# A recurrent mixer with a gated feed-forward branch: another order of transpositions, exponentials and output sums in the mixer's loop

## The chip, the cores and the metric

The kernel runs on one core of one Trainium2 chip, in float32. The metric is the device time of one launch in microseconds. Three runs of the kernel before took 1824.26, 1824.22 and 1823.35 us, so the median is 1824.22 us.

The engines are called as in the profile: PE is the matrix engine (PEld its weight loads), DVE the VectorE, ACT the ScalarE, POOL the GpSimd engine, and SP the engine that issues most DMAs. Each engine works through its own instructions in order; they wait for each other through semaphores.

## The reference

The input x has 4 batches of 256 tokens with 512 columns (1024 tokens). Cut to what matters:

```python
xn = layernorm(x)
# mixer: 128 heads of 64, 8 groups, state 128
zxbcdt = xn @ in_proj_w.T                  # gate | x,B,C | dt
gate, xBC, dt = split(zxbcdt)
xBC = silu(causal_conv(xBC, conv_w, taps=4) + conv_b)
x_, B, C = split(xBC);  dt = softplus(dt + dt_bias);  A = -exp(A_log)
# per head: y[t] = sum_{s<=t} (C[t].B[s]) * exp(sum_{s<m<=t} A*dt[m]) * dt[s] * x_[s] + D * x_[t]
y = y * silu(gate)
y = y * rsqrt(mean(y*y over the group's 1024 columns) + 1e-5) * norm_w
s = y @ out_proj_w.T
# feed-forward on the same xn, ternary weights with a scale per row
f = (silu(xn @ gate_w.T) * (xn @ up_w.T)) @ down_w.T
return x + s * silu(f)
```

The reference computes the recurrence in chunks of 32 tokens; the kernel takes chunks of 128, two per batch.

## The kernel before

**Front.** The function `front` normalizes x, transposes it, computes the feed-forward branch in 28 iterations and stores it to DRAM. Between its products it feeds in "pieces", three per iteration: the dt rows, the scores C.B of all 8 groups (`bc_pieces`, stored to `scores`), and `early_pieces`. The latter loads the two projection weight tiles of one mixer tile, waits for four turns of the pieces, adds and subtracts their blocks on DVE (`combine_to`) and stores the sums to `early` in DRAM. It does so for EARLY = 7 tiles.

**Mixer.** The 8192 channels are 64 tiles of 128 channels (two heads each), eight tiles per group. The loop at L714 has 66 steps. Step i projects tile i, finishes the y of tile i-1, gates and squares tile i-2, and computes a part of the output projection of an older group. All instructions stand in an order written out by hand (`manual_schedule`), so that the order in the program is the order on each engine's queue.

The projection of a tile uses seven products of half size instead of eight (Strassen's scheme in Winograd's form). Its left factors are blocks of the two weight tiles and sums of them (s1, s2, s4, s3); its right factors are blocks of the normalized input and sums made once (`xc`). The results gather in three PSUM banks px, pq and pz (pool `ps_proj`, three buffers). The PE order in step i is a11 (px), s1 (pq), s2 (px), a12 (pz), s3 (px), then the first transposition group, a22 (px), s4 (pq), then the second transposition group. Between the px products ACT copies px away: to pz (L750), gT (L759), and the two halves of `xpad` (L771, L806). DVE adds pq to xpad (L795) and to gT (L808). The left sums of a tile come from `early` for the first seven tiles (L841) and from `combine_w` on DVE for later ones; both go into the one buffer of the pool `scp`.

For tile i-1, `decay_scan` (DVE, L560) and `decay_exp` (ACT, L563) make the decay matrices `m` of both heads from rows loaded with DMAs; `meet` (L566, L567) multiplies them with the scores. `values_0` transposes the first chunk of each batch into the PSUM tile `tp` and multiplies it twice on DVE (L580, first with dt, then with dt_tail); `values_1` does the same with the second chunk and one multiply (L589). Both take `tp` from pool `ps_t`, which has one buffer. `y_products` (L613) then forms y.

After the taps of the convolution (L181) comes its silu (L186). For tiles below LEAD = 6 it runs on ACT in the next step, after the copy on L750, followed by both exponentials; for later tiles it ends the step itself, with the first exponential after it. Exponential and silu need different tables on ACT, so each step loads a table twice.

**Output.** Four batches of a finished group are projected by seven products of quarter size each (`out_first`), four of them in an even step and three in the next odd one, from step 10 on. The left factors come from the stored tiles (`load_gated`, pool `yap`, two buffers), with four sums on DVE (`left_factors`, L649 to L652, one buffer `sy`). ACT scales each result into `sa` or `sb` (L724), and POOL adds them into `acc` in DRAM (L857 to L860). The right factors' sums (`right_factors`, `toms`) are spread over the steps with on = 7, 0 and 1. The last group is projected after the loop: DVE adds each product to the loaded sum (L890), `end` multiplies by the feed-forward branch, adds x and stores. The four left sums for the next batch follow the last `end` of a batch.

In steps 64 and 65 there is no projection any more; the gating, the output products and the y of tile 63 remain.

Of the kernel before, what the change touches and what calls it, by code (L numbers as in the profile page):

```python
# [50 lines left out]
P = 128  # L51
NB = 4
L = 256
NC = 2
# [20 lines left out]
LEAD = 6  # L75
EARLY = 7
# [5 lines left out]
def mixer_ffn(ctx: ExitStack, tc: tile.TileContext, x, in_w, conv_w, conv_b, dt_bias, a_log, d_col,  # L82
# [23 lines left out]
    scp = main.enter_context(tc.tile_pool(name="scp", bufs=1))  # L106
# [60 lines left out]
    def by_batch(v):  # L167
        return v.rearrange("p (b l) -> p b l", l=L)
# [20 lines left out]
    def front(pre, one_of, fp, f2, hp, wq):  # L189
# [251 lines left out]
        def early_pieces():  # L441
            for n in range(EARLY):
                w = wq.tile([P, 2, KT, P], F32, name="wq")
                for m, i in enumerate((n + 1, CT + n + 1)):
                    nc.sync.dma_start(w[:, m], in_w[i])
                for _ in range(4):
                    yield
                s = wq.tile([P, 4, KT // 2, P], F32, name="sq")
                yield from combine_to(s[:, 0], s[:, 1], s[:, 2], s[:, 3], w)
                nc.sync.dma_start(early[n], s)  # L450
                yield
# [84 lines left out]
    yap = main.enter_context(tc.tile_pool(name="yap", bufs=2, reuse_waits="tile"))  # L536
# [25 lines left out]
    def decay_exp(m):  # L562
        nc.scalar.activation(m, m, AF.Exp)  # L563
# [145 lines left out]
    with tc.manual_schedule():  # L709
# [3 lines left out]
        sqacc, rs, ya, outs = None, None, None, None  # L713
        for i in range(CT + 2):  # L714
# [4 lines left out]
            sums = []  # L719
# [5 lines left out]

            if i + 1 <= EARLY:
                w = wp.tile([P, 2, KT, P], F32, name="w")
                nc.sync.dma_start(w[:, 0], in_w[i + 1])
                nc.sync.dma_start(w[:, 1, 0:2], early[i, :, 3])
                nc.sync.dma_start(w[:, 1, 2:4], in_w[CT + i + 1, :, 2:4])  # L730
            elif i + 1 < CT:
                w = load_w(i + 1, CT + i + 1)
# [18 lines left out]
            if old and i - 1 < LEAD:  # L751
                conv_silu(i - 1, xTs[i - 1])
                decay_exp(ms[i - 1][0])
            if old:
                decay_exp(ms[i - 1][1])
            if here:
                product(pq, s1, t1, True)
                product(px, s2, t2, False)
                nc.scalar.copy(gT[:, HALF:], px)  # L759
                if i:  # L760
                    decay_scan(ms[i][0])
                product(pz, a12, x21, False)
# [23 lines left out]
            if og >= 0 and on % 2 == 0:  # L786
                ob, ya = on // 2, nxt
                left, sums = left_factors(ya)
                for make in sums:
                    make()  # L790
# [3 lines left out]
            if here:  # L794
                nc.vector.tensor_add(xpad_h[1], xpad_h[1], by_batch(pq))  # L795
            if old:
                vs = values_0(i - 1, xTs[i - 1])
            if og >= 0 and on == 0:
                rs = small.tile([P, NT], F32, name="rs2", bufs=2)
                nc.vector.reciprocal(rs, sd)  # L800
            for n, turn in ((wg, PER_G - 1), (og, 0), (og, 1)):
                if n >= 0 and on == turn:
                    toms[n].pop(0)()
            if here:
                product(px, a22, t4, False)
                nc.scalar.copy(xpad_h[0], by_batch(px))  # L806
                product(pq, s4, x22, False)
                nc.vector.tensor_add(gT[:, HALF:], gT[:, HALF:], pq)  # L808
            if old:
                vs.append(values_1(i - 1, xTs[i - 1]))  # L810
            if here:
                xTs[i] = xtp.tile([P, NB, L], F32, name="xT")
                last_tap(i, xTs[i], xpad)
            if here:
                nc.scalar.activation(gT[:, 0:HALF], pz, AF.Silu)
            if og >= 0:
                if on % 2 == 0:
                    sa = osp.tile([P, NC, HID], F32, name="sa")
                    sb = osp.tile([P, 3, HH], F32, name="sb")
                    outs = out_first(left, rights[og], leave)  # L820
                for n in range(4 - on % 2):
                    next(outs)
                    if here and n == 1:
                        nc.scalar.activation(gT[:, HALF:], gT[:, HALF:], AF.Silu)
            elif here:
                nc.scalar.activation(gT[:, HALF:], gT[:, HALF:], AF.Silu)
# [7 lines left out]
            if here:  # L834
# [12 lines left out]
                if i == 0:  # L847
                    decay_scan(ms[i][0])
                decay_scan(ms[i][1])
# [26 lines left out]
        yas = {0: nxt, 1: load_gated(G - 1, 1)}  # L876
# [8 lines left out]
        for b in range(NB):  # L885
# [14 lines left out]
            sums = []  # L900
            for n, _ in enumerate(out_first(left, rights[G - 1], leave_last)):
                if n == 4:
                    end(1, slice(HH, HID))
                if n == 5:
                    end(0, slice(0, HID))
            end(1, slice(0, HH))
            if b + 1 < NB:
                left, sums = left_factors(yas[b + 1])
                for make in sums:
                    make()  # L910
            if b + 2 < NB:
                yas[b + 2] = load_gated(G - 1, b + 2)
                whole[b + 2] = fetch(b + 2)
    main.close()
# [46 lines left out]
```

## Time and profile before

| what | value |
|---|---|
| median of three runs | 1824.22 us |
| the profiled execution's own time | 1825.28 us |
| its span, from first to last instruction | 1823.6 us |
| front | about 332 us |
| steps 2 to 5 of the mixer | 17.79 us each |
| steps 7 and 8 | 19.05 and 19.04 us |
| main steps, even and odd | 23.27 and 21.55 us |
| PE busy | 1744.5 us (96%) |
| DVE busy | 1451.8 us (80%) |
| ACT busy | 1072.9 us (59%) |
| mean granted PE clock | 0.99 |

Lines of the page's groups give the line of the program, the engine, the operation, output and inputs, and then busy time, mean duration and the idle time before it. A line of the timeline gives start, duration, engine, line and the number of merged instructions; the bracket at its end tells how long the engine stood idle before it, and what ended that. The step times are the distances between the starts of the copy on L750. Busy time of PE contains overlaps of one matmul with the next, so 96% busy doesn't mean that a matmul of 512 columns takes the 0.6 us of its row: four of them start every 1.72 us.

### The profile page before, as it was taken

What the parts mean: (1) busy time and instruction counts of PE and PEld (TensorE: products, weight loads), DVE (VectorE), ACT (ScalarE), POOL (GpSimd) and SP (SyncE); (2) the same over time, 40 slices, a digit from 0 to 9 for tenths busy, and PEclk for the clock granted to TensorE, in tenths of its full rate; (3) what the DMA queues carried; (4) which work ended last, traced back from release to release, by engine and by line L of the source; (5) the groups of instructions that cost most, each with busy time, mean ns of one, the idle gap of its engine ahead of it and who ended that gap; (6) DMA issues with size and microseconds to landing.
All of it is one profiled execution on the core that took longest, in us unless ns stands there. A gap on an engine that the chain in (4) does not pass through costs nothing.

```text
span 1823.6 us, 22452 instructions
## 1 busy us (share of the span) xinstructions
PE 1744.5 (96%) x8446; PEld 1113.5 (61%) x8446; DVE 1451.8 (80%) x1736; ACT 1072.9 (59%) x1419; POOL 198.8 (11%) x235
## 2 busy tenths in 40 slices
PE   6899899899899999999999999999999999999988
PEld 4566566545456666666666666666666666666676
DVE  5556657598898888888888888888888888888866
ACT  3543333477766666666666666666666666666630
POOL 2222112000000000111011101110111011101110
PEclk8999999999999999999999999999999999999989
DMA  6235443467646665766676667666767676767665
GB/s 202 66 131 173 145 145 132 151 218 207 211 150 213 199 199 181 211 200 197 183 213 199 193 186 210 196 188 197 204 197 200 183 205 196 202 182 202 176 181 169
DMA packets 161739, 337.05 MB, mean 185 GB/s; under 512 B 15072, under 2 KB 54752, under 8 KB 161632
## 3 DMA queue, kind: packets, MB, share of 16 engines
q1 hardware_dynamic: 139120, 283.19, 44.8%
q0 software_dynamic: 22512, 52.44, 16.5%
q8 instruction: 67, 1.10, 0.2%
q14 instruction: 40, 0.33, 0.1%
HBM read 232.55 MB, written 74.19 MB: 168 GB/s over the span
## 4 chain that ended last, share of the span: by engine, by line
PE 84%; DVE 8%; ACT 6%; issue 2%; DMA 1%; SPq 0%; DVEq 0%; ACTq 0%
PE px L173 27%; PE po L669 20%; PE pq L173 12%; PE py L613 9%; PE pz L173 6%; PE pp L279 4%; ACT xpad L771 2%; PE pf L287 2%; PE tp L572 1%; PE pg L432 1%; DVE cT L181 1%; ACT m L563 1%; PE pv L631 1%; DVE xT L181 1%; DVE m L560 0%
## 5 line engine op out<-in xcount | busy, mean ns | idle before, releaser
L173 PE MATMUL px<-xc,w 128*128 128x512 f32 x576 | 279.9, 608 | 23.5 <-ACT xpad L771 15.7
L560 DVE TENSOR_TENSOR_SCAN m<-m,after 128x1024 f32<-128x1024 f32 x128 | 291.9, 2282 | 0.0
L181 DVE SCALAR_TENSOR_TENSOR xT<-xpad,cw,xT 128x1024 f32<-128x1024 f32 x192 | 246.1, 1282 | 4.6
L173 PEld LDWEIGHTS px<-xc,w 128*128 128x128 f32 x576 | 103.4, 190 | 142.5 <-issue 97.2
L669 PE MATMUL po<-wo,ya 128*128 128x256 f32 x768 | 178.3, 382 | 0.0
L613 PE MATMUL py<-m,v 128*64 128x128 f32 x2048 | 160.6, 276 | 5.3 <-DVE v L589 5.3
L566 DVE TENSOR_TENSOR m<-m,gm 128x1024 f32<-128x1024 f32 x128 | 154.8, 1210 | 6.8 <-ACT m L563 6.8
L669 PEld LDWEIGHTS po<-wo,ya 128*128 128x128 f32 x768 | 142.5, 192 | 17.6 <-issue 0.4
L831 POOL DMA_DIRECT2D sqacc<-sq x55 | 48.3, 879 | 948.9 <-ACT sq L783 948.9
L173 PE MATMUL px<-xc,s 128*128 128x512 f32 x288 | 138.1, 602 | 13.4 <-ACT cpad L402 7.2
L173 PE MATMUL px<-xnT,w 128*128 128x512 f32 x288 | 141.8, 614 | 0.0
L173 PE MATMUL pq<-xc,s 128*128 128x512 f32 x288 | 135.4, 592 | 1.6 <-DVE xT L181 1.6
L173 PE MATMUL pq<-xnT,s 128*128 128x512 f32 x288 | 135.7, 593 | 0.5 <-DVE xpad L795 0.4
L563 ACT ACTIVATE m<-m 128x1024 f32<-128x1024 f32 x128 | 134.7, 1057 | 1.7 <-DVE m L560 0.9
L173 PE MATMUL pz<-xnT,w 128*128 128x512 f32 x288 | 135.3, 592 | 0.0
L613 PEld LDWEIGHTS py<-m,v 128*64 128x64 f32 x2048 | 116.9, 137 | 27.3 <-issue 19.7
L669 PE MATMUL po<-tw,sy 128*128 128x256 f32 x512 | 117.8, 382 | 2.8 <-DVE sy L649 1.4
L808 DVE TENSOR_TENSOR gT<-gT,pq 128x512 f32<-128x512 f32 x64 | 44.0, 688 | 83.4 <-PE pq L173 83.4
L795 DVE TENSOR_TENSOR xpad<-xpad,pq 128x512 f32<-128x512 f32 x64 | 43.8, 684 | 83.3 <-ACT xpad L771 83.1
L572 PEld LDWEIGHTS tp<-ident,xT 128*128 128x128 f32 x512 | 64.1, 141 | 75.0 <-issue 75.0
L669 PEld LDWEIGHTS po<-tw,sy 128*128 128x128 f32 x512 | 97.5, 191 | 18.6 <-DVE m L890 2.8
L620 DVE TENSOR_TENSOR yg<-py,gT 128x512 f32<-128x512 f32 x128 | 83.9, 678 | 28.6 <-PE py L613 28.6
(165 smaller groups left out, 3077.5 us busy)
## 6 DMA issues: line engine op xcount, KB each, us to landing
m<-rows SPq DMA_DIRECT2D x128, 512.0 KB, 6.3
w<-in_in_w SPq DMA_DIRECT2D x137, 256.0 KB, 6.7
mo<-rows SPq DMA_DIRECT2D x128, 256.0 KB, 7.0
gated<-yg SPq DMA_DIRECT2D x64, 512.0 KB, 8.2
ya<-gated SPq DMA_DIRECT2D x31, 1024.0 KB, 7.0
sqacc<-sq POOLq DMA_DIRECT2D x55, 512.0 KB, 5.4
wo<-in_out_w SPq DMA_DIRECT2D x64, 256.0 KB, 7.1
acc<-sa POOLq DMA_DIRECT2D x24, 512.0 KB, 6.0
```

Of the source, the lines that this page charges most:

```text
L173: nc.tensor.matmul(pp, a[:, k, :], b[:, k, :], start=start and k == 0, stop=k == KT // 2 - 1, skip_group_check=not start)
L181: nc.vector.scalar_tensor_tensor(xT, xpad[:, :, k:k + L], cw[:, i, k:k + 1], xT, ALU.mult, ALU.add)
L279: nc.tensor.matmul(pp, w[:, k * P:(k + 1) * P], part[:, k, :], start=(k == 0 and part is xh), stop=(k == KT - 1 and part is xl))
L560: nc.vector.tensor_tensor_scan(m, m, after, 0.0, ALU.add, ALU.mult)
L563: nc.scalar.activation(m, m, AF.Exp)
L566: nc.vector.tensor_mul(m, m, gm[:, 0:T])
L572: nc.tensor.transpose(tp[:, b, :], xT[:, b, c * P:(c + 1) * P], ident)
L613: nc.tensor.matmul(py[d, q * P:(q + 1) * P], v[:, b, h, :], m, start=False, stop=stop, skip_group_check=True)
L620: nc.vector.tensor_mul(yg[:, 2 * i:2 * i + 2, :], ps[i], by_batch(gT[:, i * HALF:(i + 1) * HALF]))
L669: nc.tensor.matmul(po, a[:, k, :], b[:, k, :], start=start and k == 0, stop=k == HG - 1, skip_group_check=not start)
L808: nc.vector.tensor_add(gT[:, HALF:], gT[:, HALF:], pq)
L831: nc.gpsimd.dma_start(sqacc, sq, accum_op=ALU.add)
```

## The change

- LEAD goes from 6 to 9 and EARLY from 7 to 10: three more tiles get their left sums from DRAM, and three more have their silu in the next step. The pool `scp` gets two buffers. `early_pieces` waits two turns instead of four between load and sums.
- In steps 2 to 9 the second exponential of tile i-1 moves behind the copy on L759. In step 0 both scans come ahead of the add on L808 and both exponentials at the step's end; step 1 has none.
- In all steps `values_1` (second transposition group and L589) moves ahead of the product s4 and its add, and the `toms` move behind `values_1`.
- In step 64 the left sums come first, and the output products of steps 64 and 65 come ahead of `values_0`.
- In the last group the four left sums for the next batch are made one by one after the products 4 to 7 of a batch; the pool `yap` has three buffers, so that two batches' tiles are loaded ahead.

```diff
-LEAD = 6
-EARLY = 7
+LEAD = 9
+EARLY = 10
...
-    scp = main.enter_context(tc.tile_pool(name="scp", bufs=1))
+    scp = main.enter_context(tc.tile_pool(name="scp", bufs=2))
...
-                for _ in range(4):
+                for _ in range(2):
                     yield
...
-    yap = main.enter_context(tc.tile_pool(name="yap", bufs=2, reuse_waits="tile"))
+    yap = main.enter_context(tc.tile_pool(name="yap", bufs=3, reuse_waits="tile"))
...
+            def project_out(between):
+                nonlocal sa, sb, outs
+                if on % 2 == 0:
+                    sa = osp.tile([P, NC, HID], F32, name="sa")
+                    sb = osp.tile([P, 3, HH], F32, name="sb")
+                    outs = out_first(left, rights[og], leave)
+                for n in range(4 - on % 2):
+                    next(outs)
+                    if n == 1:
+                        between()
+
+            def left_sums():
+                nonlocal ob, ya, left
+                if og >= 0 and on % 2 == 0:
+                    ob, ya = on // 2, nxt
+                    left, sums = left_factors(ya)
+                    for make in sums:
+                        make()
+
+            if not here:
+                left_sums()
...
-            if old and i - 1 < LEAD:
+            lead = old and i - 1 < LEAD
+            if lead:
                 conv_silu(i - 1, xTs[i - 1])
-                decay_exp(ms[i - 1][0])
-            if old:
+                if i > 1:
+                    decay_exp(ms[i - 1][0])
+            elif old:
                 decay_exp(ms[i - 1][1])
             if here:
                 product(pq, s1, t1, True)
                 product(px, s2, t2, False)
                 nc.scalar.copy(gT[:, HALF:], px)
+                if lead and i > 1:
+                    decay_exp(ms[i - 1][1])
                 if i:
                     decay_scan(ms[i][0])
                 product(pz, a12, x21, False)
...
-            if og >= 0 and on % 2 == 0:
-                ob, ya = on // 2, nxt
-                left, sums = left_factors(ya)
-                for make in sums:
-                    make()
+            if here:
+                left_sums()
...
+            if not here:
+                project_out(lambda: None)
             if old:
                 vs = values_0(i - 1, xTs[i - 1])
...
+            if here:
+                product(px, a22, t4, False)
+                nc.scalar.copy(xpad_h[0], by_batch(px))
+            if old:
+                vs.append(values_1(i - 1, xTs[i - 1]))
             for n, turn in ((wg, PER_G - 1), (og, 0), (og, 1)):
                 if n >= 0 and on == turn:
                     toms[n].pop(0)()
             if here:
-                product(px, a22, t4, False)
-                nc.scalar.copy(xpad_h[0], by_batch(px))
+                if i == 0:
+                    decay_scan(ms[i][0])
+                    decay_scan(ms[i][1])
                 product(pq, s4, x22, False)
                 nc.vector.tensor_add(gT[:, HALF:], gT[:, HALF:], pq)
-            if old:
-                vs.append(values_1(i - 1, xTs[i - 1]))
...
-                if i == 0:
-                    decay_scan(ms[i][0])
-                decay_scan(ms[i][1])
+                if i:
+                    decay_scan(ms[i][1])
+                else:
+                    decay_exp(ms[i][0])
+                    decay_exp(ms[i][1])
...
-        yas = {0: nxt, 1: load_gated(G - 1, 1)}
+        yas = {0: nxt, 1: load_gated(G - 1, 1), 2: load_gated(G - 1, 2)}
...
             for n, _ in enumerate(out_first(left, rights[G - 1], leave_last)):
+                if n == 3 and b + 1 < NB:
+                    ahead, sums = left_factors(yas[b + 1])
+                if n >= 3 and b + 1 < NB:
+                    sums.pop(0)()
                 if n == 4:
                     end(1, slice(HH, HID))
                 if n == 5:
                     end(0, slice(0, HID))
             end(1, slice(0, HH))
-            if b + 1 < NB:
-                left, sums = left_factors(yas[b + 1])
-                for make in sums:
-                    make()
+            left = ahead
             if b + 2 < NB:
-                yas[b + 2] = load_gated(G - 1, b + 2)
                 whole[b + 2] = fetch(b + 2)
+            if b + 3 < NB:
+                yas[b + 3] = load_gated(G - 1, b + 3)
```

In the main loop with a projection (`here`), `project_out` stands where the output products stood before.

More of the change, by code (lines that the diff above doesn't have):

```diff
@@ L712, in mixer_ffn @@
         xTs, gTs, yps, wos, rights, toms = {}, {}, {}, {}, {}, {}
-        sqacc, rs, ya, outs = None, None, None, None
+        sqacc = rs = ya = outs = left = nxt = ob = sa = sb = None
         for i in range(CT + 2):
@@ L718, in mixer_ffn @@
             wg, wn = og + 1, on
-            sums = []
             def leave(po, row, col, layer):
@@ L804, in mixer_ffn @@
             if here:
-                product(px, a22, t4, False)
-                nc.scalar.copy(xpad_h[0], by_batch(px))
+                if i == 0:
+                    decay_scan(ms[i][0])
+                    decay_scan(ms[i][1])
                 product(pq, s4, x22, False)
                 nc.vector.tensor_add(gT[:, HALF:], gT[:, HALF:], pq)
-            if old:
-                vs.append(values_1(i - 1, xTs[i - 1]))
-            if here:
                 xTs[i] = xtp.tile([P, NB, L], F32, name="xT")
@@ L815, in mixer_ffn @@
                 nc.scalar.activation(gT[:, 0:HALF], pz, AF.Silu)
[L816 to L826, printed above, removed]
+                if og >= 0:
+                    project_out(lambda: nc.scalar.activation(gT[:, HALF:], gT[:, HALF:], AF.Silu))
+                else:
+                    nc.scalar.activation(gT[:, HALF:], gT[:, HALF:], AF.Silu)
             if old:
@@ L846, in mixer_ffn @@
                     ms[i + 1] = load_rows(i + 1)
-                if i == 0:
-                    decay_scan(ms[i][0])
-                decay_scan(ms[i][1])
+                if i:
+                    decay_scan(ms[i][1])
+                else:
+                    decay_exp(ms[i][0])
+                    decay_exp(ms[i][1])
             if here and i >= LEAD:
@@ L898, in end @@
                 nc.sync.dma_start(out[t * P:(t + 1) * P, cols], to)
-            sums = []
             for n, _ in enumerate(out_first(left, rights[G - 1], leave_last)):
+                if n == 3 and b + 1 < NB:
+                    ahead, sums = left_factors(yas[b + 1])
+                if n >= 3 and b + 1 < NB:
+                    sums.pop(0)()
                 if n == 4:
```

## The prediction

> **What bounds the kernel now.** I read the page first, then the waits, then the timeline of single steps. "Step i" is the value of i in the mixer's loop.
>
> The first part of the page, busy time and share of the span:
>
> ```profile
> PE 1744.5 (96%) x8446; PEld 1113.5 (61%) x8446; DVE 1451.8 (80%) x1736; ACT 1072.9 (59%) x1419; POOL 198.8 (11%) x235
> ```
>
> PE sets the time, with VectorE next. By stages: the front takes 332 us; steps 2 to 5 take 17.79 us each, 7 and 8 take 19.05; from step 10 even steps take 23.27 and odd ones 21.55 (starts of the copy on L750). Steps 10 to 63 are two thirds of the span, so I looked there for what stands between two matmuls. PE in step 32 (start, duration, instruction):
>
> ```profile
> 1022.45 1.98 PE L173 MATMUL px<-xc,w 128*128 128x512 f32 x4 [0.24 <-ACT xpad L771]
> 1024.27 1.88 PE L173 MATMUL pq<-xnT,s 128*128 128x512 f32 x4
> 1025.99 0.60 PE L572 MATMUL tp<-ident,xT 128*128 128x128 f32 x4
> ```
>
> One short wait (for the copy of px), then the product a22, the product s4, the second transposition. Nothing else in the step waits. VectorE over the same time, from the step before:
>
> ```profile
> 1004.64 0.69 DVE L808 TENSOR_TENSOR gT<-gT,pq 128x512 f32<-128x512 f32 x1 [1.87 <-PE pq L173]
> 1005.25 0.68 DVE L589 TENSOR_TENSOR v<-tp,dt 128x512 f32<-128x512 f32 x1
> ...
> 1022.96 0.68 DVE L795 TENSOR_TENSOR xpad<-xpad,pq 128x512 f32<-128x512 f32 x1
> 1023.56 0.68 DVE L580 TENSOR_TENSOR v<-tp,dt 128x512 f32<-128x512 f32 x1
> 1024.16 0.68 DVE L580 TENSOR_TENSOR v<-tp,dt_tail 128x512 f32<-128x512 f32 x1
> 1026.19 0.69 DVE L808 TENSOR_TENSOR gT<-gT,pq 128x512 f32<-128x512 f32 x1 [1.34 <-PE pq L173]
> ```
>
> No line between 1004.64 and 1024.84 shows idle time: 20.20 us of unbroken VectorE work, nearly as long as the PE's step. The last reader of the first transposition (L580, dt_tail) ends at 1024.84, after a22 has been issued (1024.27), and this costs nothing only because s4 stands ahead of the second transposition. What that wait looks like without cover is seen once in the waits (us in total, times, longest), in step 64:
>
> ```profile
> PE tp L572 <- DVE v L580: 8.2, 1, 8.2
> ```
>
> [...] the second transposition has to wait for both L580; the line above agrees. [...] the trace of before keeps program order (step 32 above). [...] after 8.2 us idle eight po matmuls take 3.62 us instead of 1.89.
>
> **The change part by part.**
>
> *Second transposition ahead of s4, all steps.* PE now runs a22, transposition, s4; VectorE runs L589 before L808 instead of after it. Nothing is added, but a wait is: the transposition for the end of L580, with s4, the output products, the y products queued behind it, and L808 and the ScalarE evictions waiting for those.
> Odd steps: L795 and a22 both start from the copy L771 (1045.71 and 1045.73 in step 33). L580 ends 1047.59, plus 0.06 to PE (the step of L795 to pq elsewhere, 506.25 to 506.31) = 1047.65; a22 makes room at 1047.55. Stall 0.10, plus about 0.08 for a restart (x4 matmuls after a wait last 1.98, not 1.88): 0.18. No faster engine elsewhere removes this, it is a race from one start.
> Even steps: from L808 of step 31 (pq start 1002.73 + 1.91) VectorE has 20.20 us, now less 0.60 for L589, which moved out of the stretch: L580 ends 1.91 + 19.60 + 0.06 = 21.57 after pq's start. PE gets there in 1024.27 − 1002.73 − 0.44 (the transposition no longer lies between) = 21.10. Stall 0.47 + 0.08 = 0.55.
> Steps that begin a group (18, 26, ... 58) have 1.8 us more of PE work (norm sums) and count as odd: there L580 is only 0.21 late by the a22 start + 1.72. So 20 even steps × 0.55 + 33 others × 0.18 = 11.0 + 5.9 = **+16** (bounds: without restart 20 × 0.47 + 33 × 0.10 = 12.7; with L589's relief gone and the lateness counted from a22 + 1.72, 20 × 0.73 + 33 × 0.21 = 21.5). The toms, now behind L589, end about when pq ends (0.65 + 0.60 + 1.17 against 0.44 + 1.88): nothing.
>
> *Steps 2 to 5.* The y products no longer wait for L589 (0.57) and s3 no longer for the second exponential (0.36 in step 2, L759). But VectorE closes a loop: L808 to the end of L580 is 15.95 unbroken (379.53 to 395.48), now 15.35; + 0.06 + 0.50 (transposition) + 1.91 (s4 to L808) = 17.82, against 17.79. The stall moves, the step stays: 0. The exponentials themselves are the same number; a switch costs one table load of 1.28 either way.
>
> *LEAD 9, EARLY 10.* Steps 6 to 8 keep the early form and lose combine_w (4 × 0.42 on VectorE) ahead. From pq of step 2 to pq of step 10 it was 149.9 (377.61 to 527.55). Now: six steps of 17.82 = 106.9; step 9 with tw1: 18.68 − 0.60 − 1.60 + 0.06 + 0.50 + 1.91 = 18.95; step 10, led by ScalarE's convolution, table, exponential, table, sd and copy as before: 20.85. Sum 146.7: **−3.2**. DMAs: three tiles load in four pieces of 896 KB instead of 512; they land in 4 to 6 us, and s (two buffers) no longer holds SP until s4 of the step (59.9 us of SP waits in L841), so the rows behind it leave earlier. Cover: rows are issued 10 us before their scans.
>
> *Front.* Three more tiles: 12 × 0.42 = 5 us of VectorE, 3 MB of DMA on SP, and only two turns (about 3.6 us each) from load to sums where the load lands in 4.2. VectorE is busy 60% there, PE 97 to 99% in most 40 us windows: mostly hidden, **+1** (0 to +5; if SP holds a load back, VectorE and PE wait).
>
> *Steps 0 and 1.* Scans and exponentials of tile 0 move into VectorE's 7.25 and 3.07 us of idle time in step 0; but the copy pz of step 1 then stands behind two exponentials. s for step 1 is issued 5 us earlier (the 1.63 wait ahead of pq ends). Followed through: pq of step 2 0.4 earlier: **−0.4** (±1).
>
> *Step 64.* The output products go ahead of the transpositions; PE idles 1737.8 to 1746.0 now. In the new order they start at 1737.3, but the second eviction writes sb, whose last store (L860) is issued 1742.54 and takes 8.4 us: s4's output product can't start before about 1751.4, PE is cold by then (3.4 instead of 1.7 us), and transpositions, values and y follow: y ends about 1760, against 1759.3. **+0.5** (−3 if the store lands at the fastest, 4.6; +2).
>
> *Last group.* Between batches PE waits 0.45 for L649 and then for L890 behind four sums:
>
> ```profile
> 1778.46 1.94 PE L669 MATMUL po<-wo,ya 128*128 128x256 f32 x8
> 1780.84 1.99 PE L669 MATMUL po<-tw,sy 128*128 128x256 f32 x8 [0.45 <-DVE sy L649]
> 1783.29 1.99 PE L669 MATMUL po<-tw,sy 128*128 128x256 f32 x8 [0.46 <-DVE m L890]
> ```
>
> From the first to the product after the third (1785.12) 6.66, unhindered 3 × 1.72 = 5.16: 1.50 lost. The sums one by one fit into VectorE's waits of 1.24, but push the evictions 5 and 6 to 1780.4 and the first of the next batch to 1782.5: 0.64 stays lost. 3 × 0.86 = **−2.6**. The third ya buffer lets loads start earlier; none was waited for.
>
> Sum: 16 − 3.2 + 1 − 0.4 + 0.5 − 2.6 = **+11.3**. The profiled span is 1823.6 (its run 1825.28), so 1834.9; the median shown, 1824.22, lies 0.6 above that span: 1835.5.
>
> **Rivals.** *The second transposition doesn't hurt* (L580 is in time, because L589 left the stretch): the rest alone gives −4.7, 1819.5, faster. It decides below 4.7 / 53 = 0.09 us per step. For it: in steps 18 to 58 of a group's start VectorE has room. Against: odd steps race from one copy and lose 0.10 by the trace. *Step 64 pays in full*: if sb is free early, y ends 7 us sooner: 1828. Against: L860's 8.4 us there, 9.0 in the median. *The upper bounds hold*: 21.5 in the main steps and the front's loads late by 3 more: 1844. For it: SP is held for up to 18 us by stores in the front. Against: PE's saturation there comes from its own work.
>
> **Chances.** Forecast 0.60, no cost of the transposition 0.10, step 64 in full 0.13, upper bounds 0.17. A change of under 0.2% (3.6 us) can't be told from none: 1820.6 to 1827.9. Faster is the first rival, 0.10; the same, the low part of step 64's case, 0.05; slower, the rest, 0.85. The range 1827 to 1845 takes in the forecast, most of the upper case and half of the step-64 case, and leaves out 0.2.
>
> **What would show it.** Right: PE waiting for L580 ahead of L572 in each main step, 0.1 in odd and about 0.5 in even ones; steps of 23.8 and 21.7 us (sum 45.6 instead of 44.82); steps 2 to 8 at about 17.8; no wait of y for L589; step 64 with ScalarE waiting for a store of sb; 12.7 instead of 13.57 us per batch at the end. Wrong: steps 10 to 63 as before, steps 2 to 8 well under 17.5, or a front longer by several us.

## The result, and the profile after

The changed kernel takes 1843.85 us (median of four runs, 1841.83 to 1846.1) against 1824.22 for the kernel before (four runs beside it, 1823.35 to 1824.26): a ratio of 1.0105, with a 95% interval of 1.009 to 1.012. It is slower by about 19.6 us, where 11.3 were forecast. The profiled run took 1842.47 us with a span of 1840.8; the span before was 1823.6.

The busy times of the kernel after, from the first part of the page, and the shares of the chain that ended last, from its fourth:

```profile
PE 1755.0 (95%) x8446; PEld 1111.1 (60%) x8446; DVE 1457.5 (79%) x1736; ACT 1072.9 (58%) x1419; POOL 200.9 (11%) x235
...
PE 59%; DVE 31%; issue 4%; ACT 3%; DMA 2%; SPq 0%; POOL 0%; DVEq 0%; ACTq 0%
```

The instruction counts are those of before; nothing was added. PE is busy 10.5 us longer with the same instructions and nearly the same mean clock (0.991 against 0.990), so the busy times don't tell where the time went. The chain is the plainest sign: before, its shares were PE 84% and DVE 8%. Now DVE has 31% of it. VectorE does hardly more than before (1457.5 against 1451.8 us), but PE now waits for it once per step.

The waits of PE after (us in total, times, longest), the lines that the change made or enlarged:

```profile
PE tp L572 <- DVE v L580: 21.1, 29, 2.5
...
PE po L669 <- ACT sb L723: 3.5, 1, 3.5
...
PE po L669 <- DVE m L911: 2.8, 1, 2.8
...
PE pv L631 <- DMA sqacc<-sq: 0.6, 1, 0.6
```

Before, the first of these was 8.2 us, once, in step 64. It now stands in 29 steps: steps 2 to 9 with 1.3 us or more each, 20 even ones of the main stretch with 0.4 (those that don't begin a group), and the tail with 1.5.

PE in step 32 after (start, duration, instruction; the bracket holds the idle time before it and what ended that), as shown for the kernel before:

```profile
1028.01 1.98 PE L173 MATMUL px<-xc,w 128*128 128x512 f32 x4 [0.24 <-ACT xpad L795]
1030.38 0.63 PE L572 MATMUL tp<-ident,xT 128*128 128x128 f32 x4 [0.39 <-DVE v L580]
1030.84 1.88 PE L173 MATMUL pq<-xnT,s 128*128 128x512 f32 x4
1032.56 1.89 PE L669 MATMUL po<-wo,ya 128*128 128x256 f32 x8
```

VectorE at the same place:

```profile
1028.95 0.68 DVE L580 TENSOR_TENSOR v<-tp,dt 128x512 f32<-128x512 f32 x1
1029.55 0.68 DVE L580 TENSOR_TENSOR v<-tp,dt_tail 128x512 f32<-128x512 f32 x1
1031.04 0.69 DVE L589 TENSOR_TENSOR v<-tp,dt 128x512 f32<-128x512 f32 x1 [0.81 <-PE tp L572]
1032.76 0.69 DVE L837 TENSOR_TENSOR gT<-gT,pq 128x512 f32<-128x512 f32 x1 [1.03 <-PE pq L173]
```

The product a22 makes room for the next at 1028.01 + 1.82 = 1029.83 (1.82 is the distance from its start to the next product in step 32 before). L580 ends at 1029.55 + 0.68 = 1030.23, the transposition starts at 1030.38. So it comes 0.55 late, 0.15 of which is the way from VectorE to PE, and s4 follows 0.46 after it instead of 0.44.

In the odd step 33 after, PE:

```profile
1051.86 1.98 PE L173 MATMUL px<-xc,w 128*128 128x512 f32 x4 [0.24 <-ACT xpad L795]
1053.87 0.63 PE L572 MATMUL tp<-ident,xT 128*128 128x128 f32 x4
1054.33 1.88 PE L173 MATMUL pq<-xnT,s 128*128 128x512 f32 x4
```

No bracket stands at the transposition, yet it starts 2.01 after a22 instead of 1.82. L580 ended there at 1053.72, 0.15 before it. This wait of about 0.2 us, short against the modelled end of the matmul ahead, has no bracket and no entry among the waits; it is found only by the distance of two starts.

**Where the time went.** The program can be cut at the starts of s4 (pq from xnT and s), which both kernels have in every step:

| stretch | before | after | difference | forecast |
|---|---|---|---|---|
| start to s4 of step 0 | 342.60 | 342.05 | -0.55 | +1 |
| to s4 of step 2 | 35.01 | 34.77 | -0.24 | -0.4 |
| to s4 of step 10 | 149.94 | 149.32 | -0.62 | -3.2 |
| to s4 of step 63 | 1199.47 | 1218.24 | +18.77 | +16 |
| to the first product of the last group | 39.21 | 38.99 | -0.22 | +0.5 |
| to the end of the span | 57.37 | 57.43 | +0.06 | -2.6 |
| sum | 1823.6 | 1840.8 | +17.2 | +11.3 |

From here on, "main stretch" is the fourth row, from s4 of step 10 to s4 of step 63, and a step's time is the distance from the s4 before to its own. Counted this way the even main steps of the kernel before take 21.55 us and the odd ones 23.27; from copy to copy it is the other way round, since the output products, which follow s4, are counted with the next step here.

### The profile page after: what moved, and what is told of

It is laid out like the page before. It is cut to its first block, busy times and chain, and to the rows that moved or that the text cites. A ratio compares the mean times of both kernels' runs of the same rounds, so it can differ in the third digit from the quotient of the medians.

```text
span 1840.8 us, 22474 instructions
## 1 busy us (share of the span) xinstructions
PE 1755.0 (95%) x8446; PEld 1111.1 (60%) x8446; DVE 1457.5 (79%) x1736; ACT 1072.9 (58%) x1419; POOL 200.9 (11%) x235
## 4 chain that ended last, share of the span: by engine, by line
PE 59%; DVE 31%; issue 4%; ACT 3%; DMA 2%; SPq 0%; POOL 0%; DVEq 0%; ACTq 0%
PE px L173 16%; PE po L669 15%; PE pq L173 10%; DVE m L560 7%; PE py L613 5%; DVE xT L181 4%; PE pz L173 4%; PE pp L279 4%; DVE m L566 3%; PE tp L572 2%; DVE v L580 2%; DVE mo L567 2%; DVE yg L620 2%; PE pf L287 2%; DVE cT L181 1%
## 5 line engine op out<-in xcount | busy, mean ns | idle before, releaser
L572 PEld LDWEIGHTS tp<-ident,xT 128*128 128x128 f32 x512 | 59.4, 142 | 106.8 <-PE px L173 53.4
L723 ACT ACTIVATE sb<-po,rs 128x256 f32<-128x256 f32 x84 | 39.8, 474 | 111.0 <-PE po L669 105.9
```

Of the source, the lines that this page charges most:

```text
L572: nc.tensor.transpose(tp[:, b, :], xT[:, b, c * P:(c + 1) * P], ident)
```

## The experiments

All eight kernels compute the whole reference. The first four were timed beside the kernel before with a median of 1822.8 us (25 runs, 1821.19 to 1826.79), the other four beside one with 1823.51 (14 runs, 1821.04 to 1826.89). Ratios are to the kernel before, with 95% intervals.

### The move alone

The kernel before, with only the second transposition moved ahead of s4 and the toms behind it:

```diff
             if here:
                 product(px, a22, t4, False)
                 nc.scalar.copy(xpad_h[0], by_batch(px))
+            if old:
+                vs.append(values_1(i - 1, xTs[i - 1]))
+            for n, turn in ((wg, PER_G - 1), (og, 0), (og, 1)):
+                if n >= 0 and on == turn:
+                    toms[n].pop(0)()
             if here:
                 product(pq, s4, x22, False)
...
-            if old:
-                vs.append(values_1(i - 1, xTs[i - 1]))
```

> The kernel before with one edit: in every step the second transposition and its multiply L589 stand ahead of the product s4, with the toms behind them, as in the changed kernel. Theory (the second transposition waits for the last reader of the first one, in the only buffer of its pool): even main steps 22.13 and odd ones 23.49 us between the starts of s4, +18.5 in all, 1842 to 1844 us. Rival (the loss belongs to other edits, such as the loads for the early tiles or the clock after step 9): under 1832 us.

Measured: 1850.2 us (1848.33 to 1850.35), ratio 1.0145 (1.013 to 1.016). The main stretch takes 1218.20, +18.73 and so the same as in the full change: even steps +0.58, odd ones +0.22. So one edit makes the whole loss there. The total is above the expectation because the steps before the main stretch, in the form of the kernel before, suffer more than I had counted: s4 of step 10 comes 7.06 later (534.61 against 527.55). Of this 0.71 is there at s4 of step 0, 1.75 comes in step 1, 0.37 in steps 2 to 6, and 4.23 in steps 7 to 10. About half of it is PE's clock: in this run the granted clock is 0.50 from 356.84 to 360.25 us, in step 1, and from 462.65 to 466.07, in step 7 (20.80 us instead of 19.04), and in the kernel before it is never below 1.00 between 316 and 1741 us. The products at the beginning of these stretches take 2.74 us, behind a wait of 1.98, and 3.29 us, behind one of 2.25, instead of 1.98. PE is busy all through both stretches, so by an estimate each loses up to half of its 3.41 us, 1.7. The waits name several further causes (L580 5.4 us in seven steps, the copy to pz 7.6 instead of 6.3, a reciprocal 1.5, a load of s 1.5), which no run separates.

### The move undone, everywhere and in the main steps only

The changed kernel with a switch around the moved part, first off in all steps, then on in steps 0 to 9 alone:

```diff
+            moved = False          # in the other kernel: moved = i < PER_G + 2
...
-            if old:
+            if old and moved:
                 vs.append(values_1(i - 1, xTs[i - 1]))
...
                 product(pq, s4, x22, False)
                 nc.vector.tensor_add(gT[:, HALF:], gT[:, HALF:], pq)
+            if old and not moved:
+                vs.append(values_1(i - 1, xTs[i - 1]))
```

The toms stand ahead of a22 again where the move is off.

> The changed kernel with this one edit undone: the second transposition and L589 behind s4 and L808 again in all steps. Theory: main steps back to 23.27 and 21.55 us, -18.8; steps 2 to 8 keep the earlier eviction to gT and lose the loop through the transposition, some 16.8 to 17.2 us each instead of 17.88, another -5 to -8; 1817 to 1821 us. Rival (other edits carry the loss): over 1830 us.

> The changed kernel with the second transposition ahead of s4 in steps 0 to 9 alone, behind it from step 10 on. Theory: the main steps' 18.8 come back and nothing else, about 1825 us, and it is slower than the kernel with the edit undone everywhere by the 5 to 8 us of steps 2 to 9. Rival (the edit pays in the first ten steps, as it takes away the wait of the y products): faster than that kernel.

Measured: 1821.4 us without the move (1818.04 to 1824.75, 12 runs), ratio 0.9991 (0.9982 to 0.9999); 1824.94 with the move in steps 0 to 9 only (1821.78 to 1827.68, 12 runs), ratio 1.001 (1.0002 to 1.0019). The main stretch goes back to 1199.36 in both, even and odd steps to 21.55 and 23.27. That confirms from the other side that the move makes the loss. Two things more follow. The move doesn't pay in the early steps either: 17.16 us each without it, 17.88 with it. And all the other parts of the change together are worth about 0.1% (0.0 to 0.2). But the kernel without the move came out a little above the 1817 to 1821 expected, and ahead of the other by 3.5 us, not by 5 to 8.

Without the move step 10 takes 25.37 us, more than the 22.57 of the full change, although nothing there was touched. PE at the start of that step:

```profile
506.35 3.17 PE L631 MATMUL pv<-one,sqacc 128*128 128x1 f32 x16 [2.77 <-DMA sqacc<-sq]
509.38 3.76 PE L173 MATMUL px<-xnT,w 128*128 128x512 f32 x4
```

The norm sums of the first group are the first PE work of step 10 and need the sum of squares from DRAM, whose last part is added by a DMA. With quicker steps ahead of it PE gets there sooner and waits 2.77 us. After that it runs at half rate, a granted clock of 0.50 from 506.76 to 513.59 us: the first product takes 3.76 instead of 1.98 us. Most of the gain of the early steps is given back right there.

### Another PSUM buffer for the second transposition

Two reasons could stand behind the loss in the main steps: the one buffer of the transposed tile, which makes PE wait for L580, or the new order of VectorE's work (L589 and the toms ahead of the add on L837). This kernel keeps the changed order and takes the buffer away as a reason: in steps 0 to 9 and in even main steps the second transposition goes to a bank of the pool of the output products, which is free at that time.

```diff
-        tp = ps_t.tile([P, NB, P], F32, name="tp", tag="t")
+        if other:
+            tp = ps_o.tile([P, NB, P], F32, name="tp", tag="o")
+        else:
+            tp = ps_t.tile([P, NB, P], F32, name="tp", tag="t")
...
-                vs.append(values_1(i - 1, xTs[i - 1]))
+                vs.append(values_1(i - 1, xTs[i - 1], here and (og < 0 or on % 2 == 0)))
```

> The changed kernel, in the same order, but the second transposition writes a bank of the output products' pool wherever this is free (steps 0 to 9 and the even main steps); in odd steps it keeps the one buffer. Theory (the buffer is the cause): even main steps lose their 0.55, some 21.55 us, odd ones stay at 23.49: -11; steps 2 to 8 fall to 16.2 to 16.6 us since nothing ties s4 to L580, -9 or so; 1820 to 1824 us. Rival (the order of L589 ahead of L808 on VectorE is the cause, whichever bank is written): 1840 us or more.

Measured: 1818.46 us (1812.96 to 1822.43, 6 runs), ratio 0.9973 (0.9956 to 0.999). Even steps take 21.55 us as before the change, odd ones, which were left alone, 23.49 as in the changed kernel; early steps take 16.37. The total is a little below the 1820 to 1824 expected. In one and the same run the steps with a second buffer lose nothing and the others keep their loss. The transpositions of the even main steps have no wait left. The groups of PE from 560 to 1000 us (busy, mean ns, then idle time ahead of the group), first the changed kernel, then this one:

```profile
L572 PE MATMUL tp<-ident,xT 128*128 128x128 f32 x152 | 23.3, 276 | 3.5 <-DVE v L580 3.2
```

```profile
L575 PE MATMUL tp<-ident,xT 128*128 128x128 f32 x155 | 23.6, 274 | 0.3
```

So in these steps the buffer is the cause, and the order of VectorE's work costs nothing that they show. That holds for the six even steps that begin a group, too: they had lost 0.22 like the odd ones (23.55 instead of 23.33), and with the second buffer they take 23.33 again. For the odd steps themselves the buffer is argued only, from the 0.15 us between the end of L580 and the transposition: no kernel here gives them a second one. The second buffer was borrowed from a pool that has a free one at that moment.

### The last group's tiles earlier

In the last group the batches follow each other every 12.09 us after the change, instead of 13.57, from the second batch on. But the first takes 16.66 instead of 12.22, and the stretch is no shorter. VectorE and SP of the changed kernel there, from the timeline:

```profile
1790.61 0.48 DVE L911 SCALAR_TENSOR_TENSOR m<-po,rs,m 128x256 f32<-128x256 f32 x1 [1.24 <-PE po L669]
1795.68 0.69 DVE L649 TENSOR_TENSOR sy<-ya 128x512 f32<-128x512 f32 x1 [4.59 <-DMA ya<-gated]
1796.29 0.48 DVE L911 SCALAR_TENSOR_TENSOR m<-po,rs,m 128x256 f32<-128x256 f32 x1
```

```profile
1781.34 8.00 SPq L640 DMA_DIRECT2D ya<-gated  x2
```

And PE:

```profile
1790.41 3.62 PE L669 MATMUL po<-wo,ya 128*128 128x256 f32 x16
1796.82 3.37 PE L669 MATMUL po<-tw,ya 128*128 128x256 f32 x8 [2.80 <-DVE m L911]
1800.03 1.89 PE L669 MATMUL po<-wo,ya 128*128 128x256 f32 x8
```

The first of the four sums now stands between two sums of a batch. It needs the second batch's tiles, whose load is issued at 1781.34 together with the third's and lands at 1795.68, 14.3 us later; L911 is queued behind it, and PE waits for L911. Before the change the same load was issued at 1764.72, took 13.6 us and was needed only at 1780.1, 15.4 us after its issue; now it is needed after 9.75 us (1795.68 − 4.59 − 1781.34). This kernel loads the tiles of the second batch at the end of step 64, with the last tile copied from SBUF later:

```diff
+            if i == CT:
+                nxt1 = load_gated(G - 1, 1, PER_G - 1)
...
-        yas = {0: nxt, 1: load_gated(G - 1, 1), 2: load_gated(G - 1, 2)}
+        yas = {0: nxt, 1: nxt1, 2: load_gated(G - 1, 2)}
...
+        nc.vector.tensor_copy(yas[1][:, PER_G - 1, :], yg[:, 1, :])
```

> The changed kernel, but the left factors of the last group's second batch are loaded at the end of step 64 (seven tiles; the eighth is copied from SBUF), before the loop's last store and the six loads of the sums. Theory (the sums one by one ask for these tiles 5 us earlier than the four sums in a row did, and their load comes too late): the 4.6 us wait of L649 and the 2.8 us wait of PE in the first batch go, with the slow matmuls behind it, -4 to -4.5 us against the changed kernel, all batches 12.1 us apart. Rival (the load is only one of several things that come late there, such as the sums from DRAM): under -1 us.

Measured: 1841.43 us (1839.29 to 1842.92, 4 runs), ratio 1.0098 (1.0083 to 1.0112). From the first product of the last group to the end of its last one it takes 48.72 us instead of 53.08: the wait is gone, as expected. But step 64 grew by 3.25. PE's waits in this kernel have

```profile
PE po L669 <- ACT sb L723: 6.4, 1, 6.4
```

where the changed kernel has 3.5. The store of sb, for whose end the next eviction waits, takes 8.33 us from its issue by POOL to the eviction (1758.40 to 1766.73) instead of 5.49 (1759.15 to 1764.64). One more load now runs beside it, of seven tiles or 896 KB, but that this load slows the store isn't shown: in the two kernels with the move undone, which don't have it, the same store took 7.96 and 7.93 us, and 5.97 in the one with another bank. The 5.49 of the changed kernel is the shortest of them. So in the two profiled executions the gain of 4.4 shrinks to about 1 us, where 4 to 4.5 were expected, and the ratios of the two kernels to the one before, 1.0098 and 1.0105, have intervals that overlap.

### The eviction buffer of step 64 apart

Step 64 in the changed kernel, PE and then ScalarE:

```profile
1755.97 1.89 PE L669 MATMUL po<-tw,sy 128*128 128x256 f32 x8
1759.67 1.99 PE L669 MATMUL po<-tw,sy 128*128 128x256 f32 x8 [1.80 <-ACT sa L723]
1765.16 3.47 PE L669 MATMUL po<-wo,sy 128*128 128x256 f32 x8 [3.50 <-ACT sb L723]
```

```profile
1764.64 0.47 ACT L723 ACTIVATE sb<-po,rs 128x256 f32<-128x256 f32 x1 [5.03 <-DMA acc<-sb]
```

The products are early, as the change wants it, and then stand still for the last store of step 63's sb. This kernel gives step 64 a buffer of its own, a weight buffer that is free by then:

```diff
-                    sb = osp.tile([P, 3, HH], F32, name="sb")
+                    if here:
+                        sb = osp.tile([P, 3, HH], F32, name="sb")
+                    else:
+                        sb = wp.tile([P, 2, KT, P], F32, name="w")
+                        sb = sb.rearrange("p a k n -> p (a k n)")[:, 0:3 * HH]
+                        sb = sb.rearrange("p (n c) -> p n c", c=HH)
```

> The changed kernel, but in step 64 the tile sb lies in a free weight buffer, so that its first write waits for no store of the step before. Theory (the earlier output products of step 64 gain nothing since ScalarE waits 5.0 us for that store, and PE then runs at half rate): no gap in PE of over 1 us between the output products of step 64, the y of tile 63 ends 5 to 6.5 us earlier, -5 to -6.5 us in all against the changed kernel. Rival (the next store or the evictions hold it just as long): under -1.5 us.

Measured: 1834.65 us (1833.46 to 1837.91, 6 runs), ratio 1.0061 (1.0048 to 1.0073). From s4 of step 63 to the end of the last y it takes 24.95 us instead of 32.07, 7.1 less. PE in step 64:

```profile
1760.36 2.00 PE L669 MATMUL po<-tw,sy 128*128 128x256 f32 x8 [1.80 <-ACT sa L723]
1762.19 1.89 PE L669 MATMUL po<-wo,sy 128*128 128x256 f32 x8
```

Some of it comes back: the last group takes 1.85 longer. PE's longest wait there is 3.0 us, where the changed kernel has 2.8; where the rest goes isn't shown. In all, the profiled execution, the slowest of the six, is 4.6 us shorter than that of the changed kernel, and the ratio is lower by 0.0044, about 8 us, where 5 to 6.5 were expected. So this edit and the one before each leave something to the other, and the last kernel makes both.

### The norm sums later

The kernel without the move, with the norm sums behind the product a12:

```diff
-            if og >= 0 and on == 0:
-                sd = norm_sums(sqacc)
...
                 product(pz, a12, x21, False)
+                if og >= 0 and on == 0:
+                    sd = norm_sums(sqacc)
```

> The kernel with the transposition back behind s4 in all steps (of the first four), and with the norm sums of a group placed behind the product a12 instead of at the start of the step. Theory (step 10 took 25.4 us there and not 21.3, since the earlier steps, now faster, run into the store of the squares on which the norm sums wait 2.8 us, and PE then goes on at half rate): step 10 about 21 to 21.5 us, -4 us against that kernel, others as they are. Rival (the half rate comes from the thin work of steps 2 to 9 and not from that wait): step 10 over 23.5 us.

Measured: 1819.32 us (1816.29 to 1820.36, 8 runs), ratio 0.9972 (0.9962 to 0.9982). Step 10 takes 21.10 instead of 25.37. The stretch from 498 to 518 us (length, then busy us and instructions of PE, PEld, DVE, ACT and POOL, the granted PE clock, the DMA share and GB/s), first without and then with this edit:

```profile
498.00:518.00 20.00, 16.48 (x88) 10.22 (x87) 15.80 (x16) 12.14 (x14) 0.00 (x0) 0.83 0.77 230
```

```profile
498.00:518.00 20.00, 17.40 (x98) 9.96 (x97) 19.60 (x23) 12.18 (x17) 0.00 (x0) 1.00 0.67 196
```

The half rate is gone (0.83 to 1.00), and with it the wait. The edit also takes the norm sums themselves, matmuls of a single column, away from that place, so it doesn't tell which of the two PE's clock answered to; what it rules out is the rival, the thin work of steps 2 to 9, which is unchanged. The ratio is lower by 0.0019 than without the edit, about 3.5 us, where 4 were expected.

### What pays, together

The changed order with the second bank in steps 0 to 9, the order of before from step 10 on, and the three edits of the last sections: norm sums later, sb apart, the second batch's tiles early.

```diff
+            moved = here and i < PER_G + 2
...
+                vs.append(values_1(i - 1, xTs[i - 1], here and og < 0))
```

> All of it: the changed kernel with the second transposition ahead of s4, and in a bank of the output pool, in steps 0 to 9 alone; behind s4 from step 10 on; norm sums later, sb apart in step 64, the second batch's tiles early. Theory: steps 2 to 8 of 16.4 us (-10 against the kernel before), step 9 at 18 (-1.4), main steps as before, step 64 -6, last group -4.4: 1797 to 1804 us. If one of the causes is wrong, its part is missing from the sum.

Measured: 1800.23 us (1799.64 to 1802.56, 4 runs), ratio 0.9875 (0.9861 to 0.9889). It beats the kernel before by 23.3 us and the changed one by more. Early steps take 16.37 us, the main stretch 1199.35, s4 of step 63 to the last y 25.55, and the batches at the end 12.1 each. With the wait for sb gone the early load does hardly any harm in step 64 (25.55 against 24.95 without it). What is left open is step 10, which takes 22.73 with a wait of 2.35 for the copy to pz and a half rate after it: the product behind the wait takes 3.61 us instead of 1.98, and the granted clock from 500 to 520 us is 0.91.

## Why the prediction was right or wrong

The forecast's sign, its main place and its mechanism were right, and 1843.85 lies inside the range of 1827 to 1845, near its upper end. The error of 8.3 us has two parts: the sum was 5.9 short (17.2 against 11.3), and the median lies 3.05 above the profiled span, not 0.6 as for the kernel before.

**The second transposition in the main steps: right in mechanism, too small in size.** Forecast were 0.55 in an even step and 0.18 in an odd one, measured 0.58 and 0.22. Two terms were off, in opposite ways. The way from the end of L580 to PE was put at 0.06, from another pair of rows; it is 0.15 in both kinds of step. The restart was put at 0.08; it is 0.02 (s4 0.46 after the transposition instead of 0.44). With these the odd step is 1053.87 − 1051.86 − 1.82 + 0.02 = 0.21, and the even one 0.55 + 0.02 = 0.57. Twenty even and 33 other steps make 11.6 + 7.3 = 18.9, close to the 18.77 measured. From copy to copy the steps take 23.86 and 21.77 us, where 23.8 and 21.7 were forecast. There is a slip as well: the terms of the prediction, 11.0 and 5.9, make 16.9, and it went on with 16. Group starts lose the same as odd steps, as assumed. Behind the waiting transposition s4 stayed in its place: in step 32 it starts 0.46 us after it (1030.38 and 1030.84).

**Steps 2 to 8: right.** 17.82 was forecast for the loop over VectorE, 17.88 measured, with PE waiting 1.3 for L580. The experiments add what I didn't ask: the same steps without the move take 17.16. "The stall moves, the step stays" was true, but the stall needn't have been there: with the second transposition in another bank the steps take 16.37. The prediction took the one buffer as given; that no other bank could be had was its author's assumption, and in these steps those of the output pool are free.

**Steps 9 and 10: the step that failed in the block of LEAD and EARLY.** Forecast 18.95 and 20.85, measured 19.43 and 22.57; this is most of the −3.2 that came out as −0.62. PE from step 9 into step 10 of the changed kernel:

```profile
502.68 1.09 PE L572 MATMUL tp<-ident,xT 128*128 128x128 f32 x4 [2.46 <-DVE v L580]
503.56 3.10 PE L173 MATMUL pq<-xnT,s 128*128 128x512 f32 x4
...
510.06 1.92 PE L631 MATMUL pv<-one,sqacc 128*128 128x1 f32 x16 [0.63 <-DMA sqacc<-sq]
511.83 2.80 PE L173 MATMUL px<-xnT,w 128*128 128x512 f32 x4
```

The wait of 2.46 us ahead of the transposition was in the sum. The half rate behind it, from 502.58 to 505.99 us (s4 3.10 instead of 1.88), was not. Nor were the wait for the last square sum and a second stretch at half rate, from 512.82 to 516.23, which lengthens the first product of step 10 (2.80 instead of 1.98) and the next one; between the two stretches the granted clock is 1.00. What brought the second on isn't shown: ahead of it PE was idle for 0.63 us only, beside the norm sums with their single columns. I had carried over the form of step 10 "as before" although its neighbour in time had changed.

**Front and steps 0 and 1: nothing to tell apart.** −0.55 and −0.24 against +1 and −0.4, within the bounds given. No load of the three more tiles was late enough to show.

**Step 64: right in mechanism, the size by luck.** The output products came early, the eviction waited for the store of sb, and PE ran at half rate behind it (3.47 us for eight matmuls instead of 1.89). −0.22 against +0.5. But the prediction counted with 8.4 us for that store, and in this execution it took 5.49. The two kernels with the move undone there have the same order in step 64 and, around s4 of step 63, that of the kernel before. Their store took 7.96 and 7.93 us, and from s4 of step 63 to the end of the last y they take 34.83 and 35.24 us, where the kernel before takes 32.30. So with a store of about 8 us the new order costs some 2.5 to 3 us in these executions, more than the +2 that the prediction gave as the bound. The kernel with a buffer of its own shows what the rival *Step 64 pays in full* would have brought: 7.1, where it said 7. The store alone stood in its way.

**The last group: wrong.** The step that failed is the sentence "The third ya buffer lets loads start earlier; none was waited for." The load of the second batch hardly starts earlier: 2.0 us ahead of the last group's first product (1781.34 and 1783.37), where it was 1.5 (1764.72 and 1766.23). It had not been waited for because it took 13.6 us and its tiles were needed 15.4 us after the issue. That left 1.8 us, and the sums that moved ahead to product 4 of the batch before ask for them 5.6 us sooner. The gain was larger than forecast, 1.5 per batch instead of 0.86, so three times 1.5; the wait of 2.80 and the half rate after it (3.37 − 1.89 = 1.48) took 4.3 of it back. A sum that moves forward needs its data earlier; I costed its VectorE time and didn't look up when the data come.

**The rivals.** *The second transposition doesn't hurt* is out by the runs with the move undone. *The upper bounds hold* gave 1844, close to the result, but not by its way: the main steps stayed under its 21.5 and the front was not late.

**The median.** The four runs of the changed kernel are 1841.83, 1842.47, 1845.22 and 1846.1 us, and their granted PE clocks 0.993, 0.991, 0.990 and 0.989. By an estimate from these clocks, with the two rates 1.00 and 0.50 of the trace, a mean clock lower by 0.004 over 1840 us is 14.7 us more at half rate, which costs 7.4 us where PE is busy all the time and less where it waits; the spread is 4.3. That fits a clock that falls in a varying number of places from run to run, but no experiment tried it, and it stays argued.

## What to carry to other kernels

An instruction moved ahead in an engine's queue is paid for by the buffer that it writes (here 0.58 us in an even main step) and by the data that it reads (here a wait of 2.80 us): look up when the last reader of the buffer ends and when the data land, and price everything that stands behind it. If the buffer is the only one of its kind, borrow another at that moment before moving anything. Short waits were worth removing here where PE fell to half rate behind them: each 3.41 us at a granted clock of 0.50 cost, by the estimate above, up to another 1.7 us. And of several waits near the end of this program removing one showed the next, so try them together.

## What the runs showed of the hardware that I had not expected

- PE fell to half rate behind waits well short of those that I had expected to matter, and of the 8.2 us in step 64 of the kernel before. Here waits of 2.46 (s4 3.10 instead of 1.88 us), 2.77 (3.76 instead of 1.98) and 2.80 us (3.37 instead of 1.89) were enough. The length of the wait alone didn't decide: in the changed kernel a wait of 2.47 us in step 1 left the rate as it was:

```profile
350.37 1.98 PE L173 MATMUL px<-xc,s 128*128 128x512 f32 x4 [2.47 <-ACT pz L770]
```

  In the changed kernel, from step 9 to the last group, the granted clock is 0.50 from 502.58, 512.82, 1765.51, 1772.34 and 1796.23 us, each time for 3.41 us, and the distances of these starts are 3, 367, 2 and 7 times 3.4133 us: in this execution they stand on one grid. In the kernel before, two stretches begin at 311.66 and 1741.84 us, 419 times 3.4133 us apart, and the second lasts 10.24 us, three times as long. The grid lay differently in two executions: the stretch ahead of the mixer, where the programs are alike, begins at 311.66 us in the kernel before and at 312.47 in the one with the move alone. In the pieces of that grid (length, then busy us and instructions of PE, PEld, DVE, ACT and POOL, the granted clock, the DMA share and GB/s) the wait of 2.47 us falls into two, the first two lines, and the one of 2.46 us almost whole into one, the third:

```profile
345.57:348.98 3.41, 2.06 (x5) 0.68 (x4) 3.34 (x4) 3.07 (x4) 0.00 (x0) 1.00 1.05 383
348.98:352.40 3.42, 2.04 (x5) 1.06 (x6) 3.42 (x3) 3.39 (x4) 0.00 (x0) 1.00 0.72 281
499.17:502.58 3.41, 1.05 (x3) 0.19 (x1) 3.36 (x5) 1.74 (x2) 0.86 (x1) 1.00 0.84 259
502.58:505.99 3.41, 3.31 (x7) 1.92 (x8) 1.82 (x2) 1.88 (x3) 0.00 (x0) 0.50 0.92 267
```

  PE was busy for 1.05 us in the third piece, and the clock was 0.50 in the next. What decides isn't shown. Busy time alone doesn't settle it: in the piece ahead of the second stretch in step 10, from 509.41 to 512.82 us, PE was busy for 2.78 us, longer than in the first two (2.06 and 2.04), behind which the clock stayed at 1.00.
- The way from the end of a VectorE multiply to the transposition that reuses its PSUM bank was 0.15 us, in step 32 and in step 33 of the changed kernel.
- One and the same accumulating store of POOL, the last of sb before step 64, took 5.49, 5.97, 7.93, 7.96 and 8.33 us from its issue to the eviction that waited for it, in five kernels; a time taken from one execution of one kernel is a poor price for it.
